# v's weights ahead of x's fourth block, and the halves of the reciprocals in a list ahead of the tiles' activations

## The chip, the cores and the metric

The kernel runs on one core of one Trainium2 chip. The time is the device time of one launch in microseconds; the figure for a kernel is the median of its runs. One further launch is recorded by the hardware profiler; all rows of a profile come from that one launch.

## The reference

One transformer layer on x of 2048 tokens by 512 channels, float32. x is one sequence of 2048 here.

```python
xn = layernorm(x)
# RWKV attention
r, v, k = split(xn @ W_rvk.T, 3)
# over the tokens t, for each channel, with w = -exp(time_decay), u = time_first:
no = max(o, u + kt);  A = exp(o - no);  Bc = exp(u + kt - no)
y  = (A * p + Bc * vt) / (A * q + Bc)
no2 = max(w + o, kt); A2 = exp(w + o - no2); B2 = exp(kt - no2)
p, q, o = A2 * p + B2 * vt, A2 * q + B2, no2
attn = (sigmoid(r) * y) @ W_out.T
# mixture of experts: 8 routed experts and 4 zero experts, the best two of a token
probs = softmax(xn @ classifier_w.T)
idx = top_k(probs + bias, 2);  rw = 1.5 * probs[idx]
ffn = sum over the two: rw * (silu(xn @ gate_e.T) * (xn @ up_e.T)) @ down_e.T
      (a zero expert gives rw * xn)
out = x + attn + ffn
```

The division in `y` and the one in the sigmoid are done together: `yT = num / ((1 + exp(-r)) * den)`. The reciprocals of the change's second part are these.

## The kernel before

The tokens are cut into four blocks (`NTB`) of 512 tokens (`TB`), the channels into four chunks (`CC`) of 128. A block and a chunk make a *unit* `(b, c)`; there are 16. The experts' tokens are gathered into 23 tiles (`TILES`) of 128, two of which are mixed from several experts.

**The head.** SyncE (SP in the profile) issues the loads in the order of the text: x's block 0, the weights for k (`load_w(2)`), the classifier's, x's blocks 1, 2 and 3 (four DMAs of 256 KB each, `load_x`), the weights for v (`load_w(1)`) and r (`load_w(0)`, 1 MB each), then small constants (`bias_sb`, `wdec`, `first_sb`) and the output weights (`wout_sb`). SP's line is in order; a DMA is issued only when the DMA eight issues earlier has landed, since the completions share eight semaphores. The stores of normalised x to the buffer `xs` come next in the same line (`store_xn`).

From `manual.enter_context(tc.manual_schedule())` on, every engine runs its instructions in the order in which the program text emits them. For each block the head emits: the norm of the *next* block (`norm(b + 1)`: statistics `st` and the scaling on VectorE, the square root `sd` and half of the scaling on ScalarE), then one step of the products (`fill(1)`: here a 128 x 512 matmul of v's first unit into the PSUM tile `pv`), the classifier's `logits`, and the transposes of the next block (`turn_block(b + 1)`: TensorE into `pt`, ScalarE copies to `xnT`). So in TensorE's line v's first matmul stands ahead of the transposes of block 1, and in ScalarE's line the copies of these stand ahead of the `sd` of block 2. Then comes the routing on VectorE (`mx` to `which_i`, `token_i`).

**The main part** is one list, `table`: every piece of work has a due position (a planner's guess, spread over the groups of products), and the pieces are emitted in the order of these positions. Four kinds of pieces share the engines:

- *products* of r, k, v for the units, in a seven-product scheme (`pair`, `sevens`; matmuls `p`, `pr`, `p2r` at line 580, adds of parts on VectorE at lines 612 and 625, postponed with `owe`);
- *tiles*: `first_half(i)` has the matmuls of the gate and up weights into the one PSUM bank `pg` (lines 1049 and 1097) and `activate(i)`: a tanh on ScalarE (`act`, line 1109) and two VectorE instructions on `act` (lines 1110, 1111), after which `pg` is free for the next tile. `second_half(i)` copies the next tile's transposed tokens (`unite`, `xgT`, from the DMA transpose `xq` that `flip` issues) and multiplies the tile before by its down weights (`finish`, `po`);
- *scans* of the units, a generator of steps: the running maximum (`obv`, line 351, with lines 353 and 354), the exponentials on ScalarE, the sums and the division's operands `er` and `num` (lines 363 to 376), then the division in two halves of 256 tokens (line 379) and the product `num * er` into `yT` (line 382). The five steps are due at 0, 5, 7.5, 12 and 14 positions after the unit's start;
- *attention*: the output projection of a token tile (`pw`, line 1230), which reads `yT`, and its VectorE step (`xrow`, line 1242).

The last block's projection, with `read_out` and the last stores, is the tail. A loop for more than 23 tiles stands ahead of it and is not entered with these inputs.

Buffers that matter: `r` tiles six (`erp`), `k` and `v` five (`kvp`), the bank `pg` one, and `ps_o` two.

Of the kernel before, what the change touches and what calls it, by code (L numbers as in the profile page):

```python
# [39 lines left out]
TB = 512  # L40
# [18 lines left out]
HALF = TB // 2  # L59
# [4 lines left out]
def layer(ctx: ExitStack, tc: tile.TileContext, x, w_rvk, w_out, decay, first, cls, ebias, gu, down, out):  # L64
    nc = tc.nc
# [30 lines left out]
    def bank(name, label, shape=(TB,)):  # L96
        return banks[name].tile([P, *shape], F32, tag=name, name=label)
# [9 lines left out]
    def load_x(b):  # L107

        if b < 3:
            t = ewp.tile([P, NJ, C], F32, tag="gw", name=f"x{b}")  # L110
        else:
            t = xyp.tile([P, NJ, C], F32, tag="xy", name=f"x{b}")
        for j in range(NJ):
            i = b * NJ + j
            nc.sync.dma_start(t[:, j, :], x[i * P : (i + 1) * P, :])
            xt[i] = t[:, j, :]
# [3 lines left out]
    def load_w(n):  # L120
        wrvk_sb[n] = keep.tile([P, CC, C], F32, tag=f"wrvk{n}", name=f"wrvk{n}")
        nc.sync.dma_start(wrvk_sb[n], w_rvk[n])
# [4 lines left out]
    nc.sync.dma_start(cls_sb, cls)  # L127
    load_x(1)
    load_x(2)
    load_x(3)  # L130
    load_w(1)
    load_w(0)
    bias_sb = const.tile([P, ET], F32, tag="bias", name="bias_sb")
    nc.sync.dma_start(bias_sb, ebias.partition_broadcast(P))
# [201 lines left out]
    def scan(b, c):  # L336

        n = f"{b}_{c}"
        s = state[c]
        w, cf = wdec[:, c : c + 1], cfac[:, c : c + 1]  # L340
        k = kvr[b, c, "k"]
        if c == 0:
            yT[b] = xyp.tile([P, CC, TB], F32, tag="xy", name=f"yT{b}")


        obv = wk1.tile([P, 3, TB + 1], F32, tag="obv", name=f"obv{n}")
        nc.vector.tensor_copy(obv[:, :, 0:1], s[:, 0:3].unsqueeze(2))
        o, bs, bvs = (obv[:, m, 0:TB] for m in range(3))
        o2, b2, bv = (obv[:, m, 1 : TB + 1] for m in range(3))

        nc.vector.tensor_tensor_scan(o2, w.to_broadcast([P, TB]), k, s[:, 0:1], ALU.add, ALU.max)  # L351
        a2 = wk1.tile([P, TB], F32, tag="a2", name=f"a2{n}")
        nc.vector.scalar_tensor_tensor(a2, o, w, o2, ALU.add, ALU.subtract)
        nc.vector.tensor_sub(b2, k, o2)
        yield
        nc.scalar.activation(a2, a2, AF.Exp)
        nc.scalar.activation(b2, b2, AF.Exp)  # L357
        yield

        v = kvr[b, c, "v"]  # L360
        sums = wk1.tile([P, 2, TB], F32, tag="sums", name=f"sums{n}")
        sq, sp = sums[:, 0, :], sums[:, 1, :]
        nc.vector.tensor_tensor_scan(sq, bs, a2, s[:, 3:4], ALU.add, ALU.mult)  # L363
        nc.vector.tensor_mul(bv, b2, v)
        nc.vector.tensor_tensor_scan(sp, bvs, a2, s[:, 4:5], ALU.add, ALU.mult)  # L365

        er = kvr[b, c, "r"]
        if b > 0:
            nc.scalar.activation(er, er, AF.Exp, scale=-1.0)
        num = yT[b][:, c, :]  # L370
        if b + 1 < NTB:
            nc.vector.tensor_copy(s[:, 0:3].unsqueeze(2), obv[:, :, TB : TB + 1])
            nc.vector.tensor_copy(s[:, 3:5].unsqueeze(2), sums[:, :, TB - 1 : TB])
        nc.vector.scalar_tensor_tensor(sq, b2, cf, sq, ALU.mult, ALU.add)
        nc.vector.scalar_tensor_tensor(er, er, 1.0, sq, ALU.add, ALU.mult)
        nc.vector.scalar_tensor_tensor(num, bv, cf, sp, ALU.mult, ALU.add)
        yield
        for hs in (slice(0, HALF), slice(HALF, TB)):
            nc.vector.reciprocal(er[:, hs], er[:, hs])  # L379
            if hs.start == 0:  # L380
                yield
        nc.vector.tensor_mul(num, num, er)
        yield

# [270 lines left out]
    units = [(b, c) for b in range(NTB) for c in range(CC)]  # L657
# [336 lines left out]
    def is_mixed(i):  # L994
        return i < TILES and seq[i] < MIXED
# [40 lines left out]
    def fetch_parts(what, i):  # L1036

        while fetched[what] < min(ahead[i] + 3, len(parts)):
            (fetch if what == "w" else fetch_down)(*parts[fetched[what]])
            fetched[what] += 1  # L1040

    def product(i, out_, lhs, rhs, c, last):

        if not is_mixed(i):
            nc.tensor.matmul(out_, lhs[:, c, :], rhs[0][:, c, :], start=(c == 0), stop=(c == last))  # L1045
            return
        for g in range(P // GROUP):
            gs = slice(g * GROUP, (g + 1) * GROUP)
            nc.tensor.matmul(
                out_[gs],  # L1050
                lhs[:, c, gs],
                rhs[g == P // GROUP - 1][:, c, :],
                start=(c == 0),
                stop=(c == last),
                tile_position=(0, g * GROUP),
            )
# [27 lines left out]
    def up(i, cs):  # L1084

        if 0 in cs:
            st[i]["pg"] = bank("gu", f"pg{i}", (2, INTER))
        pg = st[i]["pg"]
        xgT, w = st[i]["xgT"], st[i]["w"]
        for c in cs:  # L1090
            if is_mixed(i):
                product(i, pg, xgT, w, c, CC - 1)
                continue

            rs = slice(c * P, (c + 1) * P)
            for k in range(CC):
                nc.tensor.matmul(  # L1097
                    pg[:, c // IC, c % IC * P : (c % IC + 1) * P],
                    w[0][:, k, rs],
                    xgT[:, k, :],  # L1100
                    start=(k == 0),
                    stop=(k == CC - 1),
                )

    def activate(i):
        pg = st[i]["pg"]

        act = ex_p.tile([P, INTER], F32, tag="act", name=f"act{i}")
        nc.scalar.activation(act, pg[:, 0, :], AF.Tanh, scale=0.5)  # L1109
        nc.vector.scalar_tensor_tensor(act, act, 1.0, pg[:, 0, :], ALU.add, ALU.mult)  # L1110
        nc.vector.tensor_mul(act, act, pg[:, 1, :])
        st[i]["act"] = act
        if not is_mixed(i):
            st[i]["actT"] = act.rearrange("p (c t) -> p c t", c=IC)
# [36 lines left out]
    def scatter_held():  # L1151
        while held:
            held.pop()()

    def first_half(i, n):

        fetch_parts("w", i)
        up(i, (0, 1))
        if i > 0 and is_mixed(i - 1):
            turn_act(i - 1)  # L1160
        up(i, (2, 3))
        activate(i)
        if i + 4 < n:
            gather(i + 4)
        scatter_held()
# [35 lines left out]
    def accumulate():  # L1201
        for n in added:
            nc.gpsimd.dma_start(out[n * P : (n + 1) * P, :], xrows[n], accum_op=ALU.add)
        added.clear()

    def attention(b, js=range(NJ)):

        for j in js:
            i = b * NJ + j
            if i >= (NTB - 2) * NJ - 2 and (j >= 2 if i in orows else j % 2 == 1):  # L1210
                po = bank("p1", f"pw{i}")
            else:
                po = ps_o.tile([P, C], F32, tag="o", name=f"pw{i}")
            if i == NT - 1:
                for h, ph in enumerate((po, bank("p3", "pw_last"))):
                    hs = slice(h * C // 2, (h + 1) * C // 2)
                    for c in range(CC):
                        nc.tensor.matmul(
                            ph[:, : C // 2],
                            yT[b][:, c, j * P : (j + 1) * P],  # L1220
                            wout_sb[:, c, hs],
                            start=(c == 0),
                            stop=(c == CC - 1),
                        )
                        yield
                    nc.vector.tensor_add(orows[i][:, hs], orows[i][:, hs], ph[:, : C // 2])
                    nc.sync.dma_start(out[i * P : (i + 1) * P, hs], orows[i][:, hs])
                continue
            for c in range(CC):
                nc.tensor.matmul(  # L1230
                    po,
                    yT[b][:, c, j * P : (j + 1) * P],
                    wout_sb[:, c, :],
                    start=(c == 0),
                    stop=(c == CC - 1),
                )
                yield
            if i in orows:
                nc.vector.tensor_add(orows[i], orows[i], po)
                nc.sync.dma_start(out[i * P : (i + 1) * P, :], orows[i])  # L1240
            else:
                nc.vector.scalar_tensor_tensor(  # L1242
                    xrows[i], xrows[i], zw[:, i : i + 1], po, ALU.mult, ALU.add
                )
                added.append(i)
                if j % 2 == 1 and i < (NTB - 2) * NJ - 2:
                    accumulate()
# [51 lines left out]
    for m in range(groups):  # L1299
        if m in after:  # L1300
            b, j = after[m]
# [95 lines left out]
```

## Time and profile before

| | us |
|---|---|
| three runs | 364.81, 364.92, 364.18 |
| median | 364.81 |
| profiled execution, whole | 364.89 |
| its span, first to last instruction | 363.1 |
| the span, end of the last matmul | 359.6 |

The granted TensorE clock is 1.000 over the span. The profile's rows name a line of the kernel, an engine and the tiles written and read; a gap in square brackets is idle time of that engine just before the instruction, with what ended it. Where an instruction waits for several things, the last by the profile is named, so that a name can be wrong when that engine had long been done. Busy time of TensorE uses ends that are modelled.

VectorE's time by stage, from the view of windows (columns here: the stretch, TensorE busy, VectorE busy, in us):

| stretch | TensorE | VectorE |
|---|---|---|
| 0 to 83 (head, routing, first products) | 78.98 | 66.58 |
| 83 to 104 | 20.32 | 20.65 |
| 104 to 146 | 41.90 | 38.75 |
| 146 to 188 | 41.40 | 36.32 |
| 188 to 320 | 132.00 | 113.27 |
| 320 to 345.6 | 24.94 | 24.11 |
| 345.6 to 363.1 | 13.99 | 7.43 |

### The profile page before, as it was taken

The numbers are of one execution on the slowest core, as the hardware profiler recorded it, in microseconds if no ns is written. First come the engines' busy times: TensorE is split into PE (matmuls) and PEld (weight loads), VectorE is DVE, ScalarE is ACT, GpSimd is POOL, SyncE is SP. The second block draws the span as 40 slices with busy tenths as digits, with TensorE's granted clock in tenths as the row PEclk, the third lists the DMA queues.
The fourth block names the chain that finished last, engine by engine and source line by source line (L and its number), as shares of the span: only waits on it lengthen the run. The fifth ranks groups of instructions, "written<-read, shape, count | busy, mean of one in ns | idle before, by whom it ended". The sixth has DMA issues, their size and how long they took to land.

```text
span 363.1 us, 5326 instructions
## 1 busy us (share of the span) xinstructions
PE 353.5 (97%) x1850; PEld 256.4 (71%) x1850; DVE 307.1 (85%) x531; ACT 159.4 (44%) x308; POOL 91.4 (25%) x118
## 2 busy tenths in 40 slices
PE   8989999999999999999999999999999999999996
PEld 3745467899875877648867689888777888864344
DVE  5859889968999998799797699997989689979971
ACT  4457322354643556515555435556443446432000
POOL 6000300431212331221421334133332123222230
PEclk9999999999999999999999999999999999999999
DMA  7999670595879599976999977989988987934782
GB/s 275 399 364 354 238 261 0 187 324 146 249 226 262 101 364 324 263 246 149 304 249 338 277 241 179 242 239 268 304 239 226 274 161 172 327 67 58 176 131 101
DMA packets 47132, 84.46 MB, mean 233 GB/s; under 512 B 26496, under 2 KB 26880, under 8 KB 43328
## 3 DMA queue, kind: packets, MB, share of 16 engines
q1 hardware_dynamic: 39792, 64.05, 56.9%
q0 software_dynamic: 7312, 20.06, 25.1%
q8 instruction: 15, 0.25, 0.3%
q14 instruction: 13, 0.11, 0.1%
HBM read 63.25 MB, written 19.27 MB: 227 GB/s over the span
## 4 chain that ended last, share of the span: by engine, by line
PE 68%; DVE 17%; DMA 7%; ACT 3%; issue 1%; SPq 1%; DVEq 0%; ACTq 0%
PE pg L1097 18%; PE p L580 16%; PE po L1045 7%; PE pr L580 7%; PE pw L1230 6%; DVE r L379 4%; PE p L479 3%; DMA xq<-xp 3%; DMA wrvk<-in_w_rvk_dram 2%; DMA x<-in_x_dram 2%; PE pr L492 2%; PE pr L319 2%; DVE sums L365 2%; DVE sums L363 2%; PE p2r L580 1%
## 5 line engine op out<-in xcount | busy, mean ns | idle before, releaser
L1097 PEld LDWEIGHTS pg<-xgT,gw 128*128 128x128 f32 x672 | 78.2, 192 | 4.2 <-ACT xgT L1078 2.0
L1097 PE MATMUL pg<-xgT,gw 128*128 128x128 f32 x672 | 79.1, 275 | 0.7 <-ACT xgT L1078 0.6
L1133 POOL DMA_INDIRECT out_dram<-yo,to_i x23 | 41.2, 1790 | 143.9 <-ACT yo L1129 28.8
L1230 PE MATMUL pw<-wout_sb,yT 128*128 128x512 f32 x120 | 54.1, 593 | 0.7 <-DVE xrows L1242 0.5
L379 DVE RECIPROCAL r<-r 128x256 f32<-128x256 f32 x32 | 54.5, 1730 | 0.0
L1230 PEld LDWEIGHTS pw<-wout_sb,yT 128*128 128x128 f32 x120 | 22.3, 190 | 25.5 <-issue 24.8
L1045 PE MATMUL po<-dw,act 128*128 128x512 f32 x84 | 39.5, 592 | 0.0
L1003 POOL DMA_INDIRECT xg<-xs,token_i x23 | 26.8, 1167 | 44.5 <-DVE empty L951 25.2
L1109 ACT ACTIVATE act<-pg 128x256 f32<-128x256 f32 x23 | 8.8, 384 | 64.2 <-PE pg L1097 59.6
L1110 DVE SCALAR_TENSOR_TENSOR act<-act,pg 128x256 f32<-128x256 f32 x23 | 9.6, 418 | 24.0 <-ACT act L1109 23.9
L1078 ACT COPY xgT<-xq 128x1024 uint16<-128x1024 uint16 x22 | 25.5, 1161 | 3.4 <-DMA xq<-xp 3.4
L1045 PEld LDWEIGHTS po<-dw,act 128*128 128x128 f32 x84 | 16.0, 190 | 13.7 <-issue 12.7
L580 PE MATMUL p<-xnT,wrvk 128*128 128x256 f32 x96 | 24.7, 380 | 0.7 <-DVE k L612 0.7
L580 PE MATMUL p<-S,wrvk 128*128 128x256 f32 x96 | 24.8, 380 | 0.0
L580 PE MATMUL p<-S,T 128*128 128x256 f32 x96 | 24.6, 379 | 0.0
L363 DVE TENSOR_TENSOR_SCAN sums<-obv,state,a 128x512 f32<-128x512 f32 x16 | 20.5, 1279 | 4.1 <-ACT obv L357 4.0
L1070 ACT COPY xp<-xg 128x1024 uint16<-128x1024 uint16 x22 | 23.0, 1046 | 0.0
L580 PEld LDWEIGHTS p<-xnT,wrvk 128*128 128x128 f32 x96 | 18.0, 190 | 6.0 <-issue 2.6
L580 PEld LDWEIGHTS p<-S,T 128*128 128x128 f32 x96 | 18.2, 190 | 5.0 <-issue 2.9
L365 DVE TENSOR_TENSOR_SCAN sums<-obv,state,a 128x512 f32<-128x512 f32 x16 | 20.5, 1284 | 0.6
L580 PEld LDWEIGHTS p<-S,wrvk 128*128 128x128 f32 x96 | 17.9, 190 | 4.3 <-issue 1.4
L351 DVE TENSOR_TENSOR_SCAN obv<-wdec,state,k 128x512 f32<-128x512 f32 x16 | 20.4, 1277 | 0.0
(262 smaller groups left out, 575.2 us busy)
## 6 DMA issues: line engine op xcount, KB each, us to landing
gw<-in_gu_dram SPq DMA_DIRECT2D x25, 1024.0 KB
dw<-in_down_dram SPq DMA_DIRECT2D x25, 512.0 KB
x<-in_x_dram SPq DMA_DIRECT2D x16, 256.0 KB
xs<-x SPq DMA_DIRECT2D x16, 256.0 KB
wrvk<-in_w_rvk_dram SPq DMA_DIRECT2D x3, 1024.0 KB
xrow<-xs SPq DMA_DIRECT2D x8, 256.0 KB
out_dram<-xrow POOLq DMA_DIRECT2D x8, 256.0 KB, 6.9
xrows<-xs SPq DMA_DIRECT2D x8, 256.0 KB
```

Of the source, the lines that this page charges most:

```text
L351: nc.vector.tensor_tensor_scan(o2, w.to_broadcast([P, TB]), k, s[:, 0:1], ALU.add, ALU.max)
L363: nc.vector.tensor_tensor_scan(sq, bs, a2, s[:, 3:4], ALU.add, ALU.mult)
L365: nc.vector.tensor_tensor_scan(sp, bvs, a2, s[:, 4:5], ALU.add, ALU.mult)
L379: nc.vector.reciprocal(er[:, hs], er[:, hs])
L580: nc.tensor.matmul(dst, rows_(k), a[:, k, :], start=(first and k == 0), stop=(k == 1), skip_group_check=True,)
L1003: nc.gpsimd.indirect_dma_start(out=xg, out_offset=None, in_=xs, in_offset=bass.IndirectOffsetOnAxis(ap=token[:, column(i) : column(i) + 1] ...
L1045: nc.tensor.matmul(out_, lhs[:, c, :], rhs[0][:, c, :], start=(c == 0), stop=(c == last))
L1070: nc.scalar.copy(xp, st[i]["xg"].bitcast(U16).rearrange("p (c h) -> p h c", h=2))
L1078: nc.scalar.copy(xgT.bitcast(U16).rearrange("p c (t h) -> p c t h", h=2), st[i]["xq"].rearrange("p (h c) t -> p c t h", h=2),)
L1097: nc.tensor.matmul(pg[:, c // IC, c % IC * P : (c % IC + 1) * P], w[0][:, k, rs], xgT[:, k, :], start=(k == 0), stop=(k == CC - 1),)
L1133: nc.gpsimd.indirect_dma_start(out=out, out_offset=bass.IndirectOffsetOnAxis(ap=index, axis=0), in_=yo[ps], in_offset=None, compute_op=ALU ...
L1230: nc.tensor.matmul(po, yT[b][:, c, j * P : (j + 1) * P], wout_sb[:, c, :], start=(c == 0), stop=(c == CC - 1),)
```

## The change

Two edits. First, `load_w(1)` moves ahead of `load_x(3)` in SP's line. Second, a unit's two halves are no longer steps of the scan: the scan's last step puts two small functions into a list, `divisions`. Each `first_half(i)` takes up to two of them off the list and emits them just ahead of `activate(i)`; `attention` empties the list when it begins, so that `yT` is written before it is read. The last three units emit their halves at once, one per step, as before.

```diff
     load_x(1)
     load_x(2)
+    load_w(1)
     load_x(3)
-    load_w(1)
     load_w(0)
...
         nc.vector.scalar_tensor_tensor(num, bv, cf, sp, ALU.mult, ALU.add)
         yield
-        for hs in (slice(0, HALF), slice(HALF, TB)):
+        def divide(h):
+            hs = slice(h * HALF, (h + 1) * HALF)
             nc.vector.reciprocal(er[:, hs], er[:, hs])
-            if hs.start == 0:
+            if h == 1:
+                nc.vector.tensor_mul(num, num, er)
+
+        for h in range(2):
+            divisions.append(lambda h=h: divide(h))
+            if (b, c) in units[-3:]:
+                divide_some(len(divisions))
                 yield
-        nc.vector.tensor_mul(num, num, er)
-        yield
+
+
+    divisions = []
+
+    def divide_some(n):
+        for _ in range(min(n, len(divisions))):
+            divisions.pop(0)()
...
         up(i, (2, 3))
+        divide_some(2)
         activate(i)
...
     def attention(b, js=range(NJ)):
 
+        divide_some(len(divisions))
         for j in js:
```

## The prediction

> **What bounds the kernel now.** I read the page first for the shares, then the waits of TensorE, then the timeline around each wait. The page's parts 1 and 4 (busy time, and the chain that ended last):
>
> ```profile
> PE 353.5 (97%) x1850; PEld 256.4 (71%) x1850; DVE 307.1 (85%) x531; ACT 159.4 (44%) x308; POOL 91.4 (25%) x118
> PE 68%; DVE 17%; DMA 7%; ACT 3%; issue 1%; SPq 1%; DVEq 0%; ACTq 0%
> ```
>
> The chain gives VectorE (DVE) 17% and TensorE (PE) 68%, which suggests that a lighter VectorE would pay. But a chain only names one releaser per step; what a change can give back is the time in which PE stood still. The view of waits, for PE alone:
>
> ```profile
> PE pv L319 <- DMA wrvk<-in_w_rvk_dram: 1.4, 1, 1.4
> PE pk L272 <- DMA wrvk<-in_w_rvk_dram: 1.2, 1, 1.2
> PE warm L691 <- DVE ones L148: 1.1, 1, 1.1
> PE p L580 <- DVE k L612: 0.7, 1, 0.7
> PE pg L1097 <- ACT xgT L1078: 0.6, 2, 0.4
> PE pw L1230 <- DVE xrows L1242: 0.5, 1, 0.5
> PE pt L261 <- ACT x L247: 0.3, 1, 0.3
> ```
>
> That is nearly all of it (columns: total us, times, longest). Of 363.1 - 353.5 = 9.6 us without a matmul, 1.1 lie before the first and 3.5 behind the last; some 5 remain, and only 0.7 + 0.6 + 0.5 of them lie where the reciprocals are. Everything else in 363.1 us is PE at work, so the two edits are priced by what they do to these rows.
>
> A rule of the Trainium skill speaks against this reading: "Perfetto Trace Analysis", section "Identifying the Most-Contended Engine", says that matmul busy share is a poor measure of headroom, because matmuls are pipelined, and that the share of LDWEIGHTS is to be used. By that rule PE is at 71%, and 29% of 363.1 us, some 105 us, could hide small stalls that shorter VectorE delays would give back. The starts decide: four 256-wide matmuls (line 580) start 0.86 us apart at 90.80, 91.67, 92.53, 93.39, where VectorE is 4.5 us behind, and 0.86 us apart at 217.56, 218.43, 219.29 too. There is no hidden stretch in the first, so I keep the 5 us.
>
> **Part one, the weights.** The timeline of the head (start, length, engine, line, in brackets the idle time before and what ended it):
>
> ```profile
> 13.05 0.99 SPq L122 DMA_DIRECT2D wrvk<-in_w_rvk_dram  x2
> 14.39 0.33 SPq L134 DMA_DIRECT2D bias_sb<-in_ebias_dram  x1
> 15.06 0.33 SPq L136 DMA_DIRECT2D wdec<-in_decay_dram  x1
> 15.75 0.33 SPq L138 DMA_DIRECT2D first_sb<-in_first_dram  x1
> 16.42 0.33 SPq L140 DMA_DIRECT2D wout_sb<-in_w_out_dram  x1
> 20.36 1.10 PE L319 MATMUL pv<-xnT,wrvk 128*128 128x512 f32 x2 [1.43 <-DMA wrvk<-in_w_rvk_dram]
> 21.93 2.05 ACT L262 COPY xnT<-pt 128x512 f32<-128x512 f32 x4 [2.38 <-PE pt L261]
> 24.20 0.18 DVE L233 RECIPROCAL r<-sd 128x4 f32<-128x4 f32 x1 [3.71 <-ACT sd L231]
> 26.20 0.69 DVE L225 BATCH_NORM_STATS2 st<-x 128x6 f32<-128x512 f32 x1
> ```
>
> At 20.36 PE has waited 1.43 us for v's weights (`load_w(1)`). Behind that one matmul, in PE's own line, stand the transposes of x's second block; behind these the copies `xnT` on ScalarE (ACT); behind these, in ScalarE's line, the square root `sd` of the third block's norm, for which VectorE waits 3.71 us. So the whole head hangs on it.
>
> How much earlier do the weights come? SP's issues are a ladder with steps of 0.66 to 0.71 us, because each waits for the DMA eight issues back: 13.05 is the landing of x's third block, first piece; 15.06 its fourth piece; 15.75 to 17.13 the first three pieces of the fourth block. 256 KB in 0.67 us; v's 1 MB weights take the 2.5 us from about 17.8 to 20.3. Moved ahead, they are issued about 10.36 instead of 13.05 and land at 15.06 + 2.5 to 2.7 = 17.6 to 17.8. PE is free at 18.92; the first sum's PSUM bank is freed by the `k` copy at 17.63 + 0.56 = 18.19. Both are before 18.92, so the 1.43 us go entirely.
>
> What is late next: the fourth block of x lands at 20.3 instead of 17.8. VectorE asks for it at 26.20, in the new run at 26.20 - 1.43 = 24.77: 4.5 us of cover; without it each us of lateness would be one of span. ScalarE finishes its second `k` copy at 19.55 and the first new transposes are there at 21.93 - 1.43 = 20.50: no new wait. VectorE's 3.71 us become 2.28. In SP's line, `first_sb` now waits for the weights (17.7 instead of 15.75) and `wout_sb` for the fourth block's first piece (about 18.4 instead of 16.42); the transfers in flight last until about 23 (r's weights), so the queue doesn't run dry, and these two are used after 60 us. The first stores to `xs` go from 17.13 to about 19; the third and the fourth wait for what they waited for (20.3 and 23). POOL's queue isn't passed.
>
> A second rule speaks against it: "DMA: Bandwidth & Descriptors", section "Queues, rings and completion order", says that completion is not in the order of issue, even within one engine's queue. Then the weights could land together with the fourth block at 20.3, and the part would be worth 0. The ladder above is in order for nine transfers in a row, step by step; I take the 1.43.
>
> After 27 us, PE has only the waits of 0.3 us in the head and none above 0.05 us until 103.16. Its suppliers there (norms, routing, gathers, expert weights, all issued after VectorE's `which_i` and `token_i`) follow PE and VectorE, not the loads, so they move with it. Part one: **-1.43 us**, from 0 to 1.43.
>
> **Part two, the list.** It removes no work: 32 halves of 1.74 us each (`RECIPROCAL r<-r`, line 379) and the products stay. What it moves, by the order of VectorE's instructions in both programs (PE, ScalarE and POOL keep their order):
>
> - Of 16 units (block, chunk) six keep their place: (0,1), (2,1), (2,2) and the last three.
> - For eight others ((0,0), (0,2), (0,3), (1,0), (1,1), (1,3), (2,0), (3,0)) the pair of halves only goes behind other VectorE work, up to just before the next tile's activation. The set of instructions before each activation is not larger than it was, so no activation is later.
> - For (1,2) and (2,3) the second half and the product (1.67 + 0.69 = 2.36 us) go ahead of the activations of tiles 10 and 18 (counted from 0). Tile 10: VectorE idles there for 2.12 us, so it is 0.2 us later. Tile 18: VectorE goes straight from the first half (275.81 + 1.75) to the activation at 277.54, so it is 2.36 us later.
>
> Who waits for an activation: PE, for the bank `pg` of the next tile. Tile 18's ends at 278.41, the next `pg` starts at 283.80: 5.39 us of cover, 3.0 left. Tile 10: 192.97 to 198.37, 5.4, of which 5.2 are left. Cost 0 each; if the cover were gone, 2.4 us. The tightest are tiles 1 and 2 (96.78 to 98.56 and 108.58 to 110.07, 1.79 and 1.50 us), and the set before these is unchanged.
>
> The product of the last unit of block 0 comes later: after 137.07 now the next scan's 2.67 us, the halves' 3.36 and the product's 0.69 make it 143.8 instead of 141.07. The projection's matmul on that quarter of `yT` comes at 146.91 + 4 x 0.43 = 148.6; the three before it wait for nothing of this. Cover 4.9 us. The buffers of `r` (six) are asked for at least 10 us after the later release, wherever the unit is one that moved.
>
> And the gains? The 0.68 us at 103.84 wait for `k` (line 612):
>
> ```profile
> 103.84 1.13 PE L580 MATMUL p<-xnT,wrvk 128*128 128x256 f32 x4 [0.68 <-DVE k L612]
> 186.59 1.16 ACT L1078 COPY xgT<-xq 128x1024 uint16<-128x1024 uint16 x1 [3.10 <-DMA xq<-xp]
> 187.81 3.84 PE L1097 MATMUL pg<-xgT,gw 128*128 128x128 f32 x32 [0.42 <-ACT xgT L1078]
> 345.64 10.54 PE L1230 MATMUL pw<-wout_sb,yT 128*128 128x512 f32 x24 [0.55 <-DVE xrows L1242]
> ```
>
> From 82.60 to that `k` VectorE has no idle time, and the two halves of (0,0) and its product are ahead of it in both orders: it comes no earlier. The 0.42 us at 187.81 come from a DMA transpose (issued 174.72, 11.8 us), the 0.17 at 164.77 from a scan whose predecessors are the same. The 0.55 at 345.64 end VectorE's chain of the last units, which keep their order and start after PE's last `pg` (319.81). So part two: **0**, from -1.27 (0.68 + 0.17 + 0.42) upward to what the rivals say.
>
> **Sum.** The profiled execution took 364.89 us (span 363.1 and 1.79 around it), 0.08 above the median of 364.81. 364.89 - 1.43 = 363.46; against the median 363.38. I say 363.4.
>
> **The rivals.**
> - *The list frees PE too.* For: VectorE is 85% busy and has 17% of the chain, and scans start up to 4 us earlier. Against: the equal sets above. It would give 364.81 - 1.43 - 1.27 = 362.1.
> - *The weights don't land sooner, or what PE gains is asked back by the next input.* For: the second rule. Against: the ladder, and 4.5 us of cover for x. It gives 364.8.
> - *A later DMA takes more than the head gives: slower.* Place: the transpose for the tile whose matmuls start at 187.81. It stands behind two expert weights of 1 MB (issued from 168.35) and already eats 3.1 us of ScalarE and all but nothing of PE's slack: every us more is a us of span. One more 1 MB weight ahead of it, at the 249 GB/s of that slice, is 4.2 us: 364.81 - 1.43 + 4.2 = 367.6. It decides from 1.43 us of extra lateness, and is slower by over 0.2% from 2.16. Against: SP's order is unchanged and every issue there follows PE, which moves as a whole.
> - *The edit does nothing in the list*, since it would be emptied where the halves stood: refuted by the order for ten units; in time it is my forecast.
>
> **How the numbers follow.** 0.2% of 364.81, 0.73 us, is about what a measurement of this kernel can tell from no change (the three runs spread over 0.74). Head alone 0.66; list too 0.13; no gain 0.10; slower by DMA 0.11. The head alone, partly lost or measured badly, falls within 0.2% in 0.02 of its 0.66. So faster 0.77, same 0.12, slower 0.11. The range reaches from the list's 362.2 to just above no change, 364.9, and leaves out the slower rival and the far end of the faster one. The head's own range is 363.0 to 363.8.
>
> **What would show it.** Right: the wait of `pv` on `wrvk` is gone or under 0.3 us, its matmul starts about 18.9, `sd`'s wait is near 2.3, `st<-x` of the last block waits for no DMA, and the 0.7 us of `k` and the 0.4 us of `xgT` stand 1.4 us earlier with their lengths. The list: pairs of halves just ahead of `act`, with VectorE's idle time before `act` shorter, and no PE row on `act`. Wrong: a new PE row on `act L1110`, on `yT` or on x; a `pv` wait that stays; or a transpose row longer than 3.1 us on ScalarE with PE behind it.

## The result and the profile after

The kernel after takes 362.58 us (median of 6 runs, 361.88 to 363.55) against 364.87 us of the kernel before (6 runs, 364.18 to 365.08). The ratio is 0.994 (95% interval 0.9923 to 0.9957), that is 1.6 to 2.8 us less. Ratios here and below are estimated from the fast runs and need not equal the quotient of two medians; three of the runs below were slow (one of the 45 of the kernel before, two of the 21 with every transpose earlier), and they move no median by over 0.3 us. The forecast was 363.4 us. The profiled execution took 362.48 us, with a span of 360.7 and a granted clock of 1.000.

Busy time and the chain that ended last, from the page of the kernel after:

```profile
PE 354.0 (98%) x1850; PEld 256.7 (71%) x1850; DVE 306.8 (85%) x531; ACT 159.0 (44%) x308; POOL 90.3 (25%) x118
PE 73%; DVE 17%; DMA 5%; ACT 2%; issue 1%; SPq 0%; DVEq 0%; ACTq 0%
```

VectorE (DVE) is as busy as it was and has the same 17% of the chain. The view of waits, TensorE (PE) alone (total us, times, longest), shows what is gone:

```profile
PE warm L703 <- DVE ones L148: 1.1, 1, 1.1
PE p L592 <- DVE k L624: 0.7, 1, 0.7
PE pw L1244 <- DVE xrows L1256: 0.6, 1, 0.6
PE pt L261 <- ACT x L247: 0.3, 1, 0.3
PE pg L1109 <- ACT xgT L1090: 0.2, 1, 0.2
```

The rows of `pv` on `wrvk` (1.4) and of `pk` on `wrvk` (1.2) are missing, and 0.4 of the 0.6 us of `pg` on `xgT`. The row of `pk` is back, with 1.2 and 1.5 us, in two later launches of this same kernel, so the change did not remove that one. (Lines of the main part are 12 to 14 higher than in the kernel before.) The timeline of the head:

```profile
9.13 3.69 PE L272 MATMUL pk<-xnT,wrvk 128*128 128x256 f32 x16
...
9.88 0.41 SPq L122 DMA_DIRECT2D wrvk<-in_w_rvk_dram  x1
...
17.11 0.33 SPq L138 DMA_DIRECT2D first_sb<-in_first_dram  x1
17.79 0.33 SPq L140 DMA_DIRECT2D wout_sb<-in_w_out_dram  x1
18.33 1.12 PE L319 MATMUL pv<-xnT,wrvk 128*128 128x512 f32 x2
19.93 2.05 ACT L262 COPY xnT<-pt 128x512 f32<-128x512 f32 x4 [0.88 <-PE pt L261]
22.20 0.18 DVE L233 RECIPROCAL r<-sd 128x4 f32<-128x4 f32 x1 [1.64 <-ACT sd L231]
24.20 0.69 DVE L225 BATCH_NORM_STATS2 st<-x 128x6 f32<-128x512 f32 x1
```

`first_sb`, issued when the weights have landed, goes out at 17.11: so they are there before `pv` at 18.33, which has no bracket any more. ScalarE's (ACT's) copies wait 0.88 us instead of 2.38, VectorE's norm 1.64 instead of 3.71, and the last block's statistics at 24.20 wait for no DMA. Later in the same launch (timeline, the rows that answer to the four of before):

```profile
101.85 1.13 PE L592 MATMUL p<-xnT,wrvk 128*128 128x256 f32 x4 [0.68 <-DVE k L624]
184.09 1.17 ACT L1090 COPY xgT<-xq 128x1024 uint16<-128x1024 uint16 x1 [2.62 <-DMA xq<-xp]
185.31 3.84 PE L1109 MATMUL pg<-xgT,gw 128*128 128x128 f32 x32
343.15 10.54 PE L1244 MATMUL pw<-wout_sb,yT 128*128 128x512 f32 x24 [0.56 <-DVE xrows L1256]
```

Start by start, `pk` begins 0.50 us earlier than in the profile before (9.13 for 9.63) and `pv` 2.03 earlier (18.33 for 20.36). The row of `pk` in the kernel before (timeline):

```profile
9.63 3.69 PE L272 MATMUL pk<-xnT,wrvk 128*128 128x256 f32 x16 [1.16 <-DMA wrvk<-in_w_rvk_dram]
```

TensorE then runs 2.0 us ahead until 187.81, where the 0.42 us wait is gone, and 2.5 ahead from there on; the two executions differ by 2.41. So in this pair of launches there are three terms: 0.50 before either edit has acted (SyncE issues v's weights at 9.88, behind that start), 1.53 at `pv`, and 0.42 at a transpose. The experiments ask which of them belong to the change.

### The profile page after: what moved, and what is told of

It reads as the page before. It is cut to its first block, busy times and chain, and to the rows that moved or that the text cites. A ratio compares the mean times of both kernels' runs of the same rounds, so it can differ in the third digit from the quotient of the medians.

```text
span 360.7 us, 5328 instructions
## 1 busy us (share of the span) xinstructions
PE 354.0 (98%) x1850; PEld 256.7 (71%) x1850; DVE 306.8 (85%) x531; ACT 159.0 (44%) x308; POOL 90.3 (25%) x118
## 4 chain that ended last, share of the span: by engine, by line
PE 73%; DVE 17%; DMA 5%; ACT 2%; issue 1%; SPq 0%; DVEq 0%; ACTq 0%
PE pg L1109 19%; PE p L592 17%; PE po L1057 8%; PE pr L592 7%; PE pw L1244 7%; DVE r L380 4%; PE p L491 3%; DMA x<-in_x_dram 3%; DMA wrvk<-in_w_rvk_dram 2%; PE pr L504 2%; PE pr L319 2%; DVE sums L365 2%; DVE sums L363 2%; PE p2r L592 1%; PE po L1061 1%
## 5 line engine op out<-in xcount | busy, mean ns | idle before, releaser
L1145 POOL DMA_INDIRECT out_dram<-yo,to_i x23 | 40.4, 1758 | 142.9 <-ACT yo L1141 28.7
L380 DVE RECIPROCAL r<-r 128x256 f32<-128x256 f32 x32 | 53.7, 1719 | 0.0
L363 DVE TENSOR_TENSOR_SCAN sums<-obv,state,a 128x512 f32<-128x512 f32 x16 | 20.5, 1280 | 4.1 <-ACT obv L357 4.0
```

The lines of the kernel that those rows point to most:

```text
L1145: nc.gpsimd.indirect_dma_start(out=out, out_offset=bass.IndirectOffsetOnAxis(ap=index, axis=0), in_=yo[ps], in_offset=None, compute_op=ALU ...
```

## The experiments

Each kernel is set against runs of the kernel before on its own chip. Labels of theories are those of the quoted expectations.

**One edit each, and the kernel after once more.** The first kernel is the kernel before with the weights' edit alone, shown here; the second is the kernel after with this edit taken back, so that the list alone is left; the third has both.

```diff
     load_x(2)
+    load_w(1)
     load_x(3)
-    load_w(1)
```

> Only the weights' move; the halves stay steps of the scan. Theory W (all of the gain is the head, TensorE's waits on the two weights): about the whole of the changed kernel's gain, 362.3 to 363.5 us; the wait of pv on wrvk is gone. Theory L (the forecast's 1.43 us are the head and the other 0.9 us of the measured 2.3 come from the list): 363.4 us or more, and the 0.42 us wait of pg on xgT at about 187 us stays. Theory K (0.5 us of the profiled difference come from k's weights, which happened to land at 9.0 instead of 9.5 us in one profile and have nothing to do with the change): the median is 1.4 to 1.9 us below before, and the start of pk differs from profile to profile.

> Only the list; v's weights stay behind x's fourth block. Theory W and K: 364.9 us, within 0.5 us of before; pv waits 1.4 us on wrvk as before, and tiles 10 and 18 have their activation 0.8 and 2.3 us after ScalarE's part with no TensorE row on it. Theory L: 0.5 to 1 us below before (363.9 to 364.4), with the wait on xgT at about 187 us gone.

> The changed kernel as it is, on the same chip as the other three. All theories: about 362.6 us. Theory K adds: pk starts anywhere from 9.1 to 9.6 us, set by the landing of k's weights or by the copy ahead of it; the runs spread over more than the kernel before's do.

| kernel | median us (runs) | ratio to before, 95% | pk starts | pv starts | pv behind pk |
|---|---|---|---|---|---|
| before, on this chip | 365.26 (45) | | | | |
| weights alone | 362.81 (8) | 0.9954, 0.9928 to 0.998 | 9.24 | 18.39 | 9.15 |
| list alone | 364.56 (22) | 0.9981, 0.9965 to 0.9998 | 9.55 | 20.25 | 10.70 |
| both | 362.54 (6) | 0.993, 0.9904 to 0.9956 | 9.85 | 18.98 | 9.13 |

The weights' edit alone gives most of it. With the list alone the wait of `pv` stands as it was (waits of TensorE, list alone):

```profile
PE pv L319 <- DMA wrvk<-in_w_rvk_dram: 1.4, 1, 1.4
...
PE p L592 <- DVE k L624: 0.7, 1, 0.7
```

The last column of the table is the useful one: `pk` starts when k's weights have landed, which differs from launch to launch, while `pv` follows `pk` at a fixed distance of one of two sizes. The list alone has an interval of 0.1 to 1.3 us less than before, and no row of TensorE that shows where: against the profile of before its starts are the same to 0.1 us up to 187.8, where the 0.42 us wait on the transposed tokens is missing. But that wait is missing with the weights alone, too, which refutes theory L there. Theory W has the time of the weights alone. Theory K is right that `pk`'s start belongs to the launch, though 9.85 lies outside its 9.1 to 9.6, and the runs of both edits spread less (1.4 us) than those of the kernel before (6.2). The list alone, at 364.56, falls between what W and L said.

**The kernel before once more.** Nothing is edited.

> The kernel before, unchanged, one more launch. What is open: whether the 0.42 us of TensorE on the transposed tokens (pg on xgT, at 187.81 of the first profile) and the landing of k's weights (pk at 9.63) belong to the kernel or to the launch. Theory K (launch): pk starts anywhere from 9.1 to 10.0; the wait of pv on v's weights is 20.3 minus (pk's start plus 9.13 plus small), so it is smaller when pk is later, and pv starts at 20.3 to 20.4 in any case. If the 0.42 us is of the kernel, it is there again at 0.3 to 0.6; if it is of the launch, it is under 0.1 or has another length.

364.89 us (one run). `pk` starts at 10.14 and `pv` at 20.87, 10.73 behind it, as at first (20.36 - 9.63 = 10.73); the wait is 1.44 (timeline):

```profile
10.14 3.69 PE L272 MATMUL pk<-xnT,wrvk 128*128 128x256 f32 x16 [1.60 <-DMA wrvk<-in_w_rvk_dram]
...
20.87 1.10 PE L319 MATMUL pv<-xnT,wrvk 128*128 128x512 f32 x2 [1.44 <-DMA wrvk<-in_w_rvk_dram]
```

So the ladder of loads moves as a whole with k's weights, and the part of the expectation that v's weights land at 20.3 in any case is refuted. The 0.42 us wait is not there: it belongs to the launch, not to the kernel.

Over all fourteen profiles, with and without edits, `pk` starts between 8.93 and 10.37. The distance to `pv` is 10.70 to 10.86 in the five with v's weights in their old place and 9.12 to 9.20 in the eight with the new (they come in the experiments before and behind this one): 1.5 to 1.7 us is what the first edit is worth at the head. (The fourteenth has the weights the other way.)

The same profiles show what the list does inside a launch. From `pv`'s start to the end of the span these launches take:

| launch | us behind `pv`'s start |
|---|---|
| before, and before once more | 342.7 and 342.2 |
| list alone | 342.3 |
| weights alone | 342.3 |
| both, in two launches | 342.3 and 342.1 |

The 342.7 is the launch with the 0.42 us wait at 187.81. Matmul by matmul, counted from `pv`, the launch with the list alone is nowhere more than 0.23 us from the kernel before once more, and it ends level with it. A third launch of both, shown further down, takes 343.3 and has a late transpose of its own. So in these launches the list moves TensorE by 0.2 us at most, and the change is worth what the head gives. The 0.6 to 1.3 us by which the medians differ beyond that show in none of these profiles.

**The weights the other way.** v's weights behind r's.

```diff
-    load_w(1)
     load_w(0)
+    load_w(1)
```

> The kernel before with v's weights moved the other way, behind r's: they land one megabyte later, at about 23.0 instead of 20.3. Theory W (PE waits for v's weights, and everything behind that matmul moves with it): the wait of pv on wrvk grows from 1.4 to about 4.1, pv starts at about 23.0, and the time is 2.5 to 2.9 us above the kernel before, some 367.6. The rival, that the head's wait is taken up later by slack: the wait grows as much, but the time stays within 0.7 us of the kernel before.

370.76 us (4 runs), ratio 1.0155 (1.0116 to 1.0194): 5.5 us above the kernel before on this chip, twice what was expected. `pv` is late as forecast, 23.21. What was not forecast stands behind it (timeline of TensorE, then the view of windows, whose last three columns are the granted clock, the DMA share and GB/s):

```profile
23.21 2.04 PE L319 MATMUL pv<-xnT,wrvk 128*128 128x512 f32 x2 [4.29 <-DMA wrvk<-in_w_rvk_dram]
25.05 3.62 PE L261 MATMUL pt<-ident,x 128*128 128x128 f32 x16
```

```profile
20.00:22.00 2.00, 0.00 (x0) 0.00 (x0) 0.42 (x3) 0.00 (x0) 0.00 (x0) 1.00 1.10 402
22.00:24.00 2.00, 0.79 (x1) 0.51 (x2) 0.00 (x0) 0.00 (x0) 0.00 (x0) 0.64 0.96 356
24.00:26.00 2.00, 2.00 (x7) 1.17 (x6) 0.00 (x0) 0.00 (x0) 0.00 (x0) 0.50 0.98 386
26.00:28.00 2.00, 2.00 (x11) 2.00 (x10) 0.00 (x0) 1.32 (x3) 0.00 (x0) 0.50 1.06 405
```

After 4.29 us without a matmul the granted clock is 0.50, and until about 29 us the rows of TensorE take about twice as long: the sixteen transposes 3.62 us where they took 1.91. `pv` starts 2.86 us later than before, the second `pv` group (23.40) 5.77 later. The rest of the kernel keeps some 5.3 of that, and 0.7 more come from a transpose at 193.83. "The Trainium skill", page "TensorE: Matmul & The Clock Gate", section "What's actually happening", says that the array falls to half its clock after an idle window of about 3.4 us; 4.29 us is past that, and the row agrees. The span keeps more than the 2.86 us by which `pv` is later, so the rival, that slack takes it up, is refuted.

**The list from another tile on.** Is the 0.68 us wait of `p` on `k` in reach of the list at all? Here tile 1 takes nothing off it, so that its activation and `k` behind it come 4 us earlier.

```diff
-    erp = pool("er", 6)
+    erp = pool("er", 7)
...
-        divide_some(2)
+        if i > 1:
+            divide_some(2)
```

> The changed kernel with the list left alone at tile 1 and with seven r buffers instead of six: the first unit's halves go behind the k add (line 612 of before) for which TensorE waits 0.68 us. Theory: the activation of tile 1 comes about 4 us earlier, the 0.68 us row of p on k is gone, 0.7 us below the changed kernel (361.9). Rival (TensorE's wait there is made up later, or another wait takes its place): the same as the changed kernel, 362.6.

364.26 us (22 runs), 1.7 above the kernel after on the same chip: a miss. The 0.68 us are gone, and a larger wait stands 17 us later (waits, timeline and windows of this kernel):

```profile
PE pg L1109 <- DVE obv L351: 2.0, 1, 2.0
```

```profile
107.97 1.28 DVE L363 TENSOR_TENSOR_SCAN sums<-obv,state,a 128x512 f32<-128x512 f32 x1 [1.68 <-ACT obv L357]
...
118.24 0.69 DVE L637 TENSOR_TENSOR v<-v,more 128x512 f32<-128x512 f32 x1
...
119.04 0.37 ACT L620 COPY more<-p 128x256 f32<-128x256 f32 x1 [5.25 <-DVE v L637]
...
119.31 1.16 ACT L1090 COPY xgT<-xq 128x1024 uint16<-128x1024 uint16 x1
...
120.52 1.77 PE L1109 MATMUL pg<-xgT,gw 128*128 128x128 f32 x10 [1.98 <-DVE obv L351]
```

```profile
120.00:122.00 2.00, 1.48 (x10) 1.48 (x11) 1.96 (x4) 2.00 (x4) 0.00 (x0) 0.84 0.00 0
122.00:124.00 2.00, 2.00 (x11) 2.00 (x10) 2.00 (x2) 0.54 (x3) 1.70 (x1) 0.50 0.71 133
124.00:126.00 2.00, 2.00 (x16) 2.00 (x16) 1.97 (x3) 0.37 (x1) 0.98 (x1) 0.81 0.97 183
```

The row names `obv`, but the chain reads otherwise. ScalarE's copy `more` waits for the sum of `v` (L637), the copy `xgT` stands behind `more` in ScalarE's line, and `pg` (tile 4's) needs `xgT`. The same two pairs of halves stand ahead of that sum in both kernels; but here the scan (L363), now ahead of a pair, comes to its exponentials too early, and VectorE stands idle for 1.68 us where it is 0.37 in the kernel after. Counted from `pk`'s start the sum of `v` comes at 108.25 instead of 107.07. In this launch the clock fell as well, behind a stop of 1.98 us: 16 matmuls in a row lost about 0.1 us each, 1.6 in all. Most runs of this kernel have no such fall: the mean clock of 18 of the 22 is 0.998 or more, and their times still run from 363.15 to 365.14. So the fall is not what makes this kernel slower than the kernel after. The seventh buffer was not tried alone; up to the halves that are moved, TensorE's starts, counted from `pv`, are those of the kernel after.

**Half a pair.** The set ahead of tile 2's activation is left as in the kernel after; one half goes from tile 1 to tile 2. The seven buffers stay.

```diff
-        divide_some(2)
+        divide_some(1 if i == 1 else 3 if i == 2 else 2)
```

> The kernel after, but tile 1 takes one half off the list instead of two, and tile 2 takes three, so that the set of VectorE's instructions ahead of tile 2's activation is what it is in the kernel after (seven buffers for r). Tile 1's activation, the v sum, the scan and the k sum behind it come 2.4 us earlier. Theory S (a later place for a half helps only where a consumer waits, and hurts only where the set ahead of another activation grows): the 0.7 us wait of p on k is gone, no new row of 2 us appears, and the time is 0.4 to 0.7 us below the kernel after, about 362.0. The rival: VectorE idles at the scan of this stretch until ScalarE's exponentials are there, the activation of tile 2 is that much later, and a wait of about 0.5 us for pg takes the place of the one removed: the time is within 0.2 us of the kernel after.

> The kernel after, unchanged, beside the kernel that splits a pair over two tiles. 362.5, 2.0 to 2.6 us below the kernel before; the wait of pv on v's weights is gone, pv starts 9.1 to 9.2 us behind pk, and the 0.7 us wait of p on k is there.

362.62 us (17 runs) against 362.49 of the kernel after (16 runs): the same. The wait of `p` on `k` is gone and a wait of 0.63 us on `pg` has come (timeline):

```profile
116.67 0.69 DVE L637 TENSOR_TENSOR v<-v,more 128x512 f32<-128x512 f32 x1
...
117.47 0.37 ACT L620 COPY more<-p 128x256 f32<-128x256 f32 x1 [3.90 <-PE p L592]
...
117.74 1.16 ACT L1090 COPY xgT<-xq 128x1024 uint16<-128x1024 uint16 x1
...
118.95 1.27 PE L1109 MATMUL pg<-xgT,gw 128*128 128x128 f32 x9 [0.63 <-ACT xgT L1090]
```

The same stretch in the kernel after (timeline):

```profile
109.93 1.28 DVE L363 TENSOR_TENSOR_SCAN sums<-obv,state,a 128x512 f32<-128x512 f32 x1 [0.37 <-ACT obv L357]
...
116.20 0.68 DVE L637 TENSOR_TENSOR v<-v,more 128x512 f32<-128x512 f32 x1
...
116.99 0.37 ACT L620 COPY more<-p 128x256 f32<-128x256 f32 x1 [2.94 <-DVE v L637]
...
117.26 1.17 ACT L1090 COPY xgT<-xq 128x1024 uint16<-128x1024 uint16 x1
...
118.65 1.61 PE L1109 MATMUL pg<-xgT,gw 128*128 128x128 f32 x13
```

The rival has the right time and the wrong chain: VectorE idles no longer than in the kernel after (0.37 us at the scan) and tile 2's activation is in time; it is `v`, `more` and `xgT` again, with nothing late but VectorE as a whole. Counted from `pk`'s start that `v` sum comes at 106.90 here and at 107.07 in the kernel after (116.20 - 9.13): it gained 0.17 us, while TensorE asks for it some 0.85 earlier (without the wait, `p` starts 0.86 us behind the matmuls of the part before it; with the wait, 1.71). From 81 to 116 us VectorE has no other idle time than these 0.37 us in the kernel after, and in both kernels a half moved within that stretch only moved the wait.

The kernel after, in the launch profiled beside it, shows a late transpose of its own (timeline):

```profile
196.76 1.16 ACT L1090 COPY xgT<-xq 128x1024 uint16<-128x1024 uint16 x1 [2.67 <-DMA xq<-xp]
197.97 2.27 PE L1109 MATMUL pg<-xgT,gw 128*128 128x128 f32 x18 [0.84 <-ACT xgT L1090]
```

**Every transpose a tile earlier.** In the three comparisons so far the medians of before and after lie 2.3 to 2.8 us apart; the head gives 1.6. Do the late transposes make up the rest?

```diff
-        if i + 2 < n:
-            flip(i + 2)
+        if i + 3 < n:
+            flip(i + 3)
...
     flip(1)
+    flip(2)
```

> The kernel before, with every DMA transpose xq issued one tile earlier (flip(i + 3) in place of flip(i + 2)). What is to be explained: in single profiles the head gives 1.5 to 1.6 us (pv starts 10.7 us behind pk in the kernel before, 9.13 in the kernel after), but the medians lie 2.3 to 2.8 apart. Theory X (transposes): the rest are waits of TensorE on late transposes, 0.4 us in one profile of the kernel before, 1.1 with the weights moved the other way, 0.8 in one of the kernel after, none in others; they differ from launch to launch and are more frequent in the kernel before. Then this kernel's median is 0.5 to 1 us below the kernel before, no launch of it is above 366, and no row of pg on xgT by DMA stands. Theory K (the rest is elsewhere): the median is within 0.3 us of the kernel before.

> The kernel after with the same edit: every transpose issued one tile earlier. Theory X: 0 to 0.3 us below the kernel after's 362.5, some 362.3, and 1.5 to 1.8 us below the kernel before with the same edit. Theory K: it stays 2.4 to 2.8 us below that kernel.

369.32 us (6 runs) and 367.30 us (21 runs), ratios 1.0106 and 1.0061 to the kernel before: the edit costs some 4 us or more in both, so it decides nothing. No copy `xgT` waits for a transpose any more, but with one buffer for `xp` the copy into it waits for the transpose before, and ScalarE's line waits behind it (timeline of the kernel after with this edit):

```profile
81.56 1.04 ACT L1082 COPY xp<-xg 128x1024 uint16<-128x1024 uint16 x1 [5.12 <-DMA xq<-xp]
...
84.52 0.70 PE L592 MATMUL p<-S,T 128*128 128x256 f32 x2 [1.80 <-ACT k L611]
```

**Two transposes a tile earlier.** The same for tiles 10 and 11 alone, with two buffers for `xp`.

```diff
-        if i + 2 < n:
+        if i + 2 < n and i not in (8, 9):
             flip(i + 2)
         if i > 0:
             finish(i - 1)
+        if i in (7, 8):
+            flip(i + 3)
...
-        xp = wk1.tile([P, 2, C], U16, tag="xp", name=f"xp{i}")
+        xp = ex_p.tile([P, 2, C], U16, tag="xp", name=f"xp{i}")
```

> The kernel before, in which only the transposes of tiles 10 and 11 (counted from 0) are issued one tile earlier, with two buffers for xp, so that no copy into xp waits for the transpose before it. Theory X (TensorE's waits on these two late transposes are what lies between 1.6 us and the medians): no wait of pg on xgT by DMA, median 364.3 to 364.7, and few launches above 366. Theory K: the median stays at 365.2 and the launches spread as widely as before. If the copies into xp block ScalarE for late gathers, a new row of TensorE behind ScalarE shows it, and the test is void.

> The kernel after with the same edit for tiles 10 and 11. Theory X: 362.2 to 362.5, 1.6 to 2.1 us below the kernel before with this edit. Theory K: 362.5, and 2.4 to 2.8 us below it.

| kernel | median us (runs) | lowest to highest | ratio to before, 95% |
|---|---|---|---|
| before, on this chip | 364.68 (30) | 363.68 to 368.61 | |
| before, two transposes earlier | 364.68 (14) | 363.81 to 365.78 | 0.999, 0.9968 to 1.0011 |
| after, two transposes earlier | 362.87 (16) | 362.19 to 363.31 | 0.9943, 0.9926 to 0.996 |

The edit does its work: `xgT` of tiles 10 and 11 waits for nothing, and TensorE has no new wait above 0.2 us. First `pv` with the old order of loads, then with the new (timelines):

```profile
19.79 1.10 PE L319 MATMUL pv<-xnT,wrvk 128*128 128x512 f32 x2 [1.57 <-DMA wrvk<-in_w_rvk_dram]
```

```profile
19.09 1.02 PE L319 MATMUL pv<-xnT,wrvk 128*128 128x512 f32 x2
```

With the edit in both, the change is worth 364.68 - 362.87 = 1.81 us, near the head's 1.6. But the kernel after without the edit was not run on this chip, and the kernel before without it has the same 364.68, some 0.5 us less than on the other chips. So it stays open whether the edit brought the difference down or the chip did. The other half of theory X fails outright: the median of before doesn't fall with the edit, and the kernel after is at 362.87, where 362.2 to 362.5 was expected. No run of the edited kernels is above 366. For the kernel after that says nothing, since none of its 28 runs without the edit is either; of the kernel before 3 of the 30 beside them are above 366 (11 of 45, 5 of 32 and 5 of 26 on the other chips), so that none in 14 can be chance. That late transposes make the long runs, or the difference between the rows and the medians, is not shown.

None of these versions is shown to beat the kernel after.

## Why the prediction was right, point by point

**The bound.** Right. The waits of TensorE, not VectorE's 17% of the chain, said what could be had: VectorE's busy time is unchanged, and within a launch the time fell by what left the list of waits. The experiments with worse orders show the same from the other side. The prediction had asked whether the 29% of the span without a weight load could take up stalls. At `pv` they do not: 2.86 us of lateness cost 5.5, the fall of the clock included.

**Part one, -1.43 us.** Right in mechanism. The weights landed at 17.11 in the profiled launch, some 0.6 before the forecast 17.6 to 17.8, of which 0.50 is that launch's earlier ladder; `pv` is bounded by TensorE itself. The second rule's worst case, weights landing together with x's fourth block, did not come: `first_sb` goes out at 17.11, and `pv` waits for no weights in any of the eight profiles with the new order. The term is 1.5 to 1.7 us, by the distance of `pv` from `pk`. The term that was mis-sized, by 0.1 to 0.3 us, is the idle time of 1.43: it starts from a modelled end of the matmul before, and without the wait `pv` follows up to 0.2 us closer. The same holds for the 0.68 us of `p`, worth 0.85 by the starts. The forecast start "about 18.9" was counted in that launch's clock; relative to `pk` it is 9.3, measured 9.12 to 9.20. The fourth block of x had its cover. VectorE's wait for `sd` was forecast at 2.28 and is 1.64: in this launch `sd` comes 2.0 us earlier and not 1.43, since `pk` had started 0.50 earlier.

**Part two, 0.** Right within a launch, open for the median. The equal sets held: no row of TensorE on `act`, and the 0.68, 0.17 and 0.55 us stay. Tile 18's activation is later as worked out, behind both halves and the product (timeline of the kernel after):

```profile
273.31 3.36 DVE L380 RECIPROCAL r<-r 128x256 f32<-128x256 f32 x2
276.70 0.69 DVE L382 TENSOR_TENSOR yT<-yT,r 128x512 f32<-128x512 f32 x1
277.31 0.42 DVE L1122 SCALAR_TENSOR_TENSOR act<-act,pg 128x256 f32<-128x256 f32 x1
```

It was 277.54 before, and TensorE is 2.5 us further on here, so it is 2.3 us later against TensorE, where 2.36 was forecast; 3.1 us of cover are left. Behind `pv` the launch with the list alone ends level with the kernel before once more. But its median is 0.1 to 1.3 us below before. One difference can be named, and it is thin: ScalarE's wait for tile 10's transpose, from which TensorE has some 2.65 us of slack, is 2.62 to 3.80 us in four profiles without the list (3.10, 2.62, 2.72, 3.80) and 0.71 to 2.62 in six with it (2.62, 1.74, 0.71, 1.18, 1.76, 2.58), whatever else these kernels change. What in the list would bring this transpose forward was not found, and launches differ by as much as the two groups do.

**The 0.42 us of `xgT`, forecast to stand with its length.** Wrong in kind. The prediction took a wait in one profile for a property of the kernel; in a second launch of the same kernel it is not there. The same holds for `pk`'s start.

**The tightest cover.** The prediction called tiles 1 and 2 the tightest, with 1.79 and 1.50 us; it counted activations alone. A tighter place lies on another way to `pg`: tile 4's `xgT`, held by the sum of `v` and the copy `more`, ends at 118.43 in the kernel after (117.26 + 1.17), and that `pg` starts at 118.65. The slack is 0.2 us, and the two kernels that hold the list back fell into it. The change itself leaves the work ahead of that sum as it was, so the forecast did not suffer.

**The sum and the rivals.** 363.4 was forecast, 362.58 came. Of the 0.8 us between them the head's term explains 0.1 to 0.3; the rest shows in no profile, and its cause is open. The head's own range was 363.0 to 363.8, and the median lies below it: it falls within the stated range because that had been widened for the list, and the list is not seen to do it. To that extent the number was luck; the mechanism of the head was not. The rival "the list frees PE too", 362.1, has the size but not the rows: its 0.68 us did not move, and the 0.42 us went without the list too. The slower rival, a later transpose at 187.81, is not seen: SyncE's order is unchanged there and moved with TensorE, as argued.

## What to carry to other kernels

Take the gain of an edit from the idle time of the engine that hardly rests, at the place of the edit. Measure it as a distance between two starts in the same launch, not as a start in one launch against a start in another; and count the rest of the launch from the later of the two, which tells whether anything else moved. Before counting the slack of a postponed instruction, follow every consumer through the in-order lines of the other engines; the nearest one by name may not be the tightest. A wait for a DMA that is there in one profile needs a second profile of the same kernel before it is called the kernel's.

## What the runs showed of the hardware that was not expected

A stop of TensorE can cost more than its length. After 4.29 us without a matmul the granted clock was 0.50 for some 6 us, and the loss grew from 2.9 to 5.8 us. In one launch windows of 0.84, 0.50 and 0.81 and about 1.6 us more came behind a stop of 1.98 us. That stop is shorter than the idle window of 3.4 us that the page on the clock gate gives; here the measurement decides. It is one launch, though: the kernel before has launches with a mean clock of 0.994 and 0.995 as well, of which no profile was kept, so that the stop caused the fall is not shown. Stops of 1.4 to 1.6 us in the head and one of 1.80 us in another kernel kept 1.00. The landing of the first weights moves from launch to launch (`pk` at 8.93 to 10.37, 1.4 us) and takes the whole ladder of loads with it. One DMA transpose of 128 x 1024 two-byte values, issued behind two expert weights of 1 MB, took some 11.8 us in the profile before (issued at 174.72, read at 186.59); the median of the 22 in the kernel after is 4.6.
